# Linear attention and the first half of an FFN in a written order of single steps, and two roots of a double norm as one power

## The chip, the cores and the metric

The kernel runs on one core of one Trainium2 chip. The metric is the time of one execution in microseconds (us). Lower is better. All data are fp32 unless a name says otherwise.

## The reference

The reference is a decoder of two layers over x of 2 x 1024 rows of 256 features: linear attention with an FFN, attention of a short context over the rows' latents, a recurrent cell, causal self-attention, cross-attention, and a mixture of experts. The change lies in the first of these, which is this:

```python
x = x + _L0_attn_ref(_layernorm(x, axis=-1), ...)       # two normalisations follow each other

def _L0_attn_ref(x, ...):
    h = layer_norm(x, ln1_g, ln1_b)                      # (x - mu) * rsqrt(var + 1e-5) * g + b
    q, k, v = heads(h @ wq), heads(h @ wk), heads(h @ wv)    # 4 heads of 64
    q = softmax(q * 64**-0.25, axis=-1)                  # over the 64 features
    k = softmax(k * 64**-0.25, axis=-2)                  # over the 1024 rows
    context = einsum('bhnd,bhne->bhde', k, v)
    x = x + merge(einsum('bhnd,bhde->bhne', q, context)) @ wo + bo
    h = layer_norm(x, ln2_g, ln2_b)
    x = x + gelu(h @ w_ff1 + b_ff1) @ w_ff2 + b_ff2      # 256 -> 1024 -> 256
    return x @ w_d + b_d
```

The double norm needs for each row the factor 1/sqrt(var + eps), called r, and for the second norm 1/sqrt(var * r * r + eps). The product of both is rr, the factor with which the attention's input is scaled.

## The kernel before

The rows of x lie on chip in four blocks of 512 rows (g = 0 to 3; blocks 0 and 1 are batch 0, blocks 2 and 3 batch 1), each as [128, 4, 256]. SP issues the loads in this order: x blocks 0 and 1, the half of w_lin with wk and wv, x blocks 2 and 3, the other half of w_lin (wq, wo), two rows of biases, w_ffn, more rows, and the weights of the two stages after.

`Linear` does the first stage. For each block: `norm` takes statistics on VectorE (`ln_stats`), gets the two roots as powers of -0.5 on POOL (`rsqrt`) with four small VectorE products around the second, writes xh = (x - mean) * rr, turns it by TensorE transposes (`turned`), and scales it into hT, one half on VectorE and the other on ScalarE (`affine`). It also writes h0 = (x - mean) * r, the residual of the attention. For each batch: `keys` multiplies, takes the maximum on VectorE and the exponential on ScalarE into kT; `values` multiplies and copies; `queries` does, for each of two halves, multiply, maximum, subtract, exponential (ScalarE), sum, reciprocal, multiply into the tile qe, then transposes and copies into qT. `context` turns kT back into rows (kr, L353), multiplies it with the values (L363), copies the blocks of the heads into cbd, and multiplies by wo (L375) into wc. `attend` multiplies qT by wc (L393) and adds to h0. `front` is the second norm and its transposes into hT2; `back` is the FFN: eight products of 512 columns each way in four pairs (L441, L427) with Gelu between (L448), the residual (L459), the copy oT (L465), the product with w_d (L474) and the sums into x (L470 for the bias, L482 for the product).

The PSUM memory is handed out as two tiles "s" of 1024 columns, two tiles "t" of 512, and one "f" of 1024. In SBUF, hT, kT and qT share four buffers ("long"); xh, qe and kr share three ("rows4").

What sets the order: the framework plans each engine's instructions itself, except inside a block `tc.manual_schedule()`, where the order of the program is kept. `linear.attention` (batch 0 and 1 up to the attention, and the FFN of block 0), the constants and first loads of `Latent` (the next stage), and `linear.rest` (FFN of block 1 and `front` of blocks 2 and 3) are planned. From then on a manual block follows: `back(2)` and `back(3)`, each alternating step by step with the text and the first batch of `Latent` (`text`, whose first tile is cr, L580 to L649, and `prepare`, whose statistics are at L664). The Latent stage's attention begins after it, with the L769 products. In the planned part the trace has VectorE at block 2's statistics before the second root's small products of block 0.

Of the kernel before, what the change touches and what calls it, by code (L numbers as in the profile page):

```python
# [25 lines left out]
P = 128  # L26
# [197 lines left out]

class Linear:
# [7 lines left out]

    def __init__(self, k, x, w, pool):

        self.k, self.x, self.pool, self.w = k, x, pool, w
        self.h0 = pool.tile([P, NT, D], F32, tag="h0", bufs=1, name="h0")
        self.hT, self.kT, self.vr, self.qT, self.wc, self.ffT = {}, {}, {}, {}, {}, {}

    def long(self, name):  # L240
        return self.own.tile([P, DC, N], F32, tag="long", bufs=4, name=name)

    def four(self, name):
        return self.pool.tile([P, 1024], F32, tag="four", bufs=5, name=name)

    def rows4(self, name):
        return self.own.tile([P, 1024], F32, tag="rows4", bufs=3, name=name)

    def turned(self, rows, out, put):

        k = self.k
        for kc in range(DC):
            tb = k.t()
            for i in range(4):
                k.nc.tensor.transpose(tb[:, i * P : (i + 1) * P], rows[:, i, kc * P : (kc + 1) * P], k.ident)
            put(out[:, kc, :], tb, kc)

    def norm(self, b, half):

        k, x = self.k, self.x  # L260
        g = 2 * b + half
        if half == 0:
            self.hT[b] = self.long("hT")
        rows = lambda i: x[:, 4 * g + i, :]
        mv, r, rr = k.ln_stats(rows, 4, twice=True)
        xh = self.rows4("xh").rearrange("p (t d) -> p t d", d=D)
        for i in range(4):
            k.ln_apply(xh[:, i, :], rows(i), mv, rr, i)
        self.turned(
            xh, self.hT[b][:, :, half * 512 : (half + 1) * 512],  # L270
            lambda out, in_, kc: k.affine(out, in_, k.vec("ln1_g", kc), k.vec("ln1_b", kc), kc),
        )
        for i in range(4):
            k.ln_apply(self.h0[:, 4 * g + i, :], rows(i), mv, r, i)

    def keys(self, b):

        k, nc, w = self.k, self.k.nc, self.w
        scale = 64.0 ** -0.25
        hT = self.hT[b]  # L280
        kT = self.kT[b] = self.long("kT")
        for mc in range(DC):
            s = k.s()
            for nb in range(2):
                for kc in range(DC):
                    nc.tensor.matmul(
                        s[:, nb * 512 : (nb + 1) * 512],
                        lhsT=w["wk"][:, kc, mc * P : (mc + 1) * P],
                        rhs=hT[:, kc, nb * 512 : (nb + 1) * 512],
                        start=(kc == 0),  # L290
                        stop=(kc == DC - 1),
                    )
            m = k.small([P, 1], "k_m")
            nc.vector.tensor_reduce(m, s, AX.X, ALU.max, negate=True)
            nc.vector.tensor_scalar_mul(m, m, scale)
            nc.scalar.activation(
                kT[:, mc, :], s, AF.Exp, bias=m, scale=scale, accum_out=self.ksum[:, b, mc : mc + 1]
            )
        nc.vector.reciprocal(self.ksum[:, b, :], self.ksum[:, b, :])

    def rows_of(self, b, g, name):

        k = self.k
        s = k.s()
        for i in range(4):
            at = (4 * g + i) * P
            for kc in range(DC):
                k.nc.tensor.matmul(
                    s[:, i * D : (i + 1) * D],
                    lhsT=self.hT[b][:, kc, at : at + P],  # L310
                    rhs=self.w[name][:, kc, :],
                    start=(kc == 0),
                    stop=(kc == DC - 1),
                )
        return s

    def values(self, b):
        vr = self.vr[b] = self.own.tile([P, TB, D], F32, tag="vr", bufs=2, name="vr")
        for g in range(2):
            s = self.rows_of(b, g, "wv")  # L320
            self.k.nc.scalar.copy(vr[:, 4 * g : 4 * g + 4, :].rearrange("p t d -> p (t d)"), s)

    def queries(self, b):

        k, nc = self.k, self.k.nc
        scale = 64.0 ** -0.25
        qT = self.qT[b] = self.long("qT")
        for g in range(2):
            s = self.rows_of(b, g, "wq").rearrange("p (h d) -> p h d", d=64)
            qe = self.rows4("qe")  # L330
            q3 = qe.rearrange("p (h d) -> p h d", d=64)
            m, sm = k.small([P, 16], "q_m"), k.small([P, 16], "q_s")
            nc.vector.tensor_reduce(m, s, AX.X, ALU.max)
            nc.vector.tensor_tensor(q3, s, m.unsqueeze(2).to_broadcast([P, 16, 64]), ALU.subtract)
            nc.scalar.activation(qe, qe, AF.Exp, scale=scale)
            nc.vector.tensor_reduce(sm, q3, AX.X, ALU.add)
            nc.vector.reciprocal(sm, sm)
            nc.vector.tensor_tensor(q3, q3, sm.unsqueeze(2).to_broadcast([P, 16, 64]), ALU.mult)
            self.turned(
                qe.rearrange("p (t d) -> p t d", d=D), qT[:, :, g * 512 : (g + 1) * 512],  # L340
                lambda out, in_, kc: k.evac(out, in_),
            )

    def context(self, b):

        k, nc, w = self.k, self.k.nc, self.w
        c, kT, vr = self.cbd[b], self.kT[b], self.vr[b]
        krs = []
        for at in range(0, TB, 4):
            s = k.s()  # L350
            for i in range(4):
                for mc in range(DC):
                    nc.tensor.transpose(  # L353
                        s[:, (i * DC + mc) * P : (i * DC + mc + 1) * P],
                        kT[:, mc, (at + i) * P : (at + i + 1) * P], k.ident,
                    )
            kr = self.rows4("kr")
            k.evac(kr, s)
            krs.append(kr.rearrange("p (t d) -> p t d", d=D))
        t = k.t()  # L360
        for pr in range(DC):
            for i in range(TB):
                nc.tensor.matmul(  # L363
                    t[:, pr * P : (pr + 1) * P],
                    lhsT=vr[:, i, pr * P : (pr + 1) * P],
                    rhs=krs[i // 4][:, i % 4, pr * P : (pr + 1) * P],
                    start=(i == 0),
                    stop=(i == TB - 1),
                )
        for hh in range(2):  # L370
            sl = slice(hh * 64, hh * 64 + 64)
            nc.vector.tensor_copy(c[sl, :, sl], t[sl, : DC * P].rearrange("p (r d) -> p r d", r=DC)[:, :, sl])
        t = k.t()
        for pr in range(DC):
            nc.tensor.matmul(  # L375
                t[:, pr * D : (pr + 1) * D], lhsT=c[:, pr, :], rhs=w["wo"][:, pr, :], start=True, stop=True
            )
        wc = self.wc[b] = self.own.tile([P, DC, D], F32, tag=f"wc{b}", bufs=1, name=f"wc{b}")
        sums = self.ksum[:, b, :]
# [6 lines left out]
    def attend(self, b):  # L386
        k, nc = self.k, self.k.nc
        for g in range(2):
            s = k.s()
            for i in range(4):  # L390
                at = (4 * g + i) * P
                for pr in range(DC):
                    nc.tensor.matmul(  # L393
                        s[:, i * D : (i + 1) * D],
                        lhsT=self.qT[b][:, pr, at : at + P],
                        rhs=self.wc[b][:, pr, :],
                        start=(pr == 0),
                        stop=(pr == DC - 1),
                    )
            four = self.h0[:, 8 * b + 4 * g : 8 * b + 4 * g + 4, :].rearrange("p t d -> p (t d)")  # L400
            nc.vector.tensor_add(four, four, s)

    def front(self, g):

        k = self.k
        h0 = self.h0[:, 4 * g : 4 * g + 4, :]
        rows = lambda i: h0[:, i, :]
        mv, r = k.ln_stats(rows, 4)
        xh = self.four("xh").rearrange("p (t d) -> p t d", d=D)
        for i in range(4):  # L410
            k.ln_apply(xh[:, i, :], rows(i), mv, r, i)
        hT = self.ffT[g] = self.four("hT2").rearrange("p (c n) -> p c n", c=DC)
        self.turned(
            xh, hT, lambda out, in_, kc: k.affine(out, in_, k.vec("ln2_g", kc), k.vec("ln2_b", kc), kc)
        )
# [1995 lines left out]
```

## Time and profile before

| | us |
|---|---|
| median of three runs | 1771.98 |
| lowest and highest of the three | 1766.24 and 1774.56 |
| the profiled execution, its own time | 1776.51 |
| span in the profile, first to last instruction | 1774.4 |
| first TensorE instruction | 13.99 |
| first product of back(2) | 191.17 |
| first product of the Latent attention (L769) | 299.51 |

The profile shows one execution. PE is TensorE's products, PEld its weight loads, DVE is VectorE, ACT ScalarE, POOL GpSimd, SP the engine that issues most loads. An fp32 product has two records on PE, a transpose has one. In the rows of order in time, brackets hold the engine's idle time before the row and what ended it. In the row PEclk, each digit is the granted TensorE clock in a fortieth of the span, in tenths of full speed. In a table of stretches, each row gives the stretch, its length, then for each engine the busy time and the number of instructions, then the granted clock (1.00 is full), the share of the DMA engines that is busy, and GB/s.

### The profile page before, as it was taken

The page shows a single profiled execution, that of the slowest core. Times are in us where ns is not written, and L with a number is a line of the kernel's source. Part 1 is how long each engine was busy: PE and PEld are TensorE (multiplying, and loading weights), DVE is VectorE, ACT ScalarE, POOL GpSimd, SP SyncE. Part 2 cuts the span into 40 slices and gives each one's busy share as a digit, 9 for nine tenths or more (in the row PEclk, how much of TensorE's full clock was granted, in tenths as well). Part 3 has the DMA queues.
Part 4 walks back from the last instruction along what each step waited for, and adds up shares of the span by engine and source line. Part 5 has one row for each costly group of instructions (what it writes and reads, how often), then busy time and mean ns, then how long its engine had stood idle before and what let it go on. Part 6 is the DMA issues. An engine that isn't in the chain of part 4 may idle for free. (4 is left out here: it accounts for less than half of the span.)

```text
span 1774.4 us, 20965 instructions
## 1 busy us (share of the span) xinstructions
PE 1677.3 (95%) x8686; PEld 882.8 (50%) x8686; DVE 804.1 (45%) x1470; ACT 512.7 (29%) x870; POOL 265.7 (15%) x298
## 2 busy tenths in 40 slices
PE   6889899999999799989999999989899999999998
PEld 4655455343343446543433443456546645665566
DVE  5532224845653524467566667366641131111222
ACT  1221232233324132325555445533121111111110
POOL 2010131133213300203111111220000000000420
PEclk9889999999999899969999999999899999999999
DMA  5000000000000100000000000050003122322321
GB/s 225 1 3 1 0 1 4 1 0 1 1 1 1 36 1 0 31 1 1 1 1 1 1 1 1 1 195 2 1 0 107 69 74 71 107 92 81 100 68 48
DMA packets 30550, 59.16 MB, mean 33 GB/s; under 512 B 3640, under 2 KB 23672, under 8 KB 30072
## 3 DMA queue, kind: packets, MB, share of 16 engines
q1 hardware_dynamic: 25512, 50.46, 8.2%
q0 software_dynamic: 1536, 4.20, 0.9%
q10 hardware_dynamic: 3408, 3.17, 0.5%
q8 instruction: 69, 1.13, 0.3%
q14 instruction: 25, 0.20, 0.0%
HBM read 51.00 MB, written 6.82 MB: 33 GB/s over the span
## 5 line engine op out<-in xcount | busy, mean ns | idle before, releaser
L2149 PE MATMUL ps_s<-pair,w 128*128 128x512 f32 (+1 forms) x704 | 304.8, 592 | 0.2 <-ACT pair L2098 0.2
L2149 PEld LDWEIGHTS ps_s<-pair,w 128*128 128x128 f32 (+1 forms) x704 | 130.9, 187 | 164.4 <-issue 163.3
L1338 ACT ACTIVATE pT<-ps_t 128x512 f32<-128x512 f32 (+3 forms) x344 | 150.6, 490 | 149.5 <-PE ps_t L1303 147.7
L1228 PE MATMUL ps_s<-kT,qT 32*128 32x512 f32 (+3 forms) x768 | 182.1, 571 | 10.3 <-DVE part L1244 6.4
L1303 PE MATMUL ps_t<-qT,kT 32*128 32x512 f32 (+3 forms) x688 | 184.3, 554 | 2.2 <-ACT pT L1338 2.2
L2158 DVE TENSOR_TENSOR hid<-ga,ps_s 128x512 f32<-128x512 f32 (+1 forms) x88 | 60.5, 687 | 272.8 <-ACT ga L2157 272.8
L2164 PE MATMUL ps_o<-wo,hid 128*128 128x256 f32 (+1 forms) x704 | 153.5, 379 | 0.0
L1244 DVE TENSOR_REDUCE part<-ps_s 128x2 f32<-128x1024 f32 (+3 forms) x128 | 130.5, 1024 | 45.4 <-PE ps_t L1303 37.3
L2164 PEld LDWEIGHTS ps_o<-wo,hid 128*128 128x128 f32 (+1 forms) x704 | 133.8, 190 | 22.0 <-issue 4.1
L2157 ACT ACTIVATE ga<-ps_s 128x512 f32<-128x512 f32 (+1 forms) x88 | 52.5, 597 | 246.5 <-PE ps_s L2149 246.5
L1228 PEld LDWEIGHTS ps_s<-kT,qT 32*128 32x128 f32 x768 | 61.4, 194 | 86.8 <-issue 46.6
L1268 PE MATMUL ps_o<-pT,vr 128*32 128x256 f32 (+4 forms) x1408 | 99.5, 361 | 1.8 <-POOL pT L1296 1.5
L1296 POOL TENSOR_SCALAR_AFFINE_SELECT pT<-pT 128x256 f32<-128x256 f32 x128 | 51.9, 407 | 319.4 <-ACT pT L1338 310.3
L910 ACT ACTIVATE pT<-ps_s 128x1024 f32<-128x1024 f32 x64 | 65.5, 1023 | 115.4 <-PE ps_s L903 115.4
L2182 POOL DMA_INDIRECT found<-eo_rows,index x32 | 31.9, 997 | 422.5 <-DMA eo_rows<-rows 387.9
L798 DVE TENSOR_REDUCE part<-ps_s 128x2 f32<-128x1024 f32 x64 | 76.4, 1218 | 28.4 <-PE ps_s L791 27.7
L1236 DVE TENSOR_TENSOR ps_s<-ps_s,causal 128x256 f32<-128x256 f32 x128 | 54.9, 429 | 66.5 <-PE ps_t L1303 44.5
L915 POOL TENSOR_TENSOR acc<-acc,pT 128x1024 f32<-128x1024 f32 x24 | 59.4, 2476 | 160.0 <-ACT pT L910 157.3
L1268 PEld LDWEIGHTS ps_o<-pT,vr 128*32 128x32 f32 x1408 | 28.9, 109 | 98.4 <-issue 84.5
L1303 PEld LDWEIGHTS ps_t<-qT,kT 32*128 32x128 f32 x688 | 71.3, 191 | 12.1 <-ACT pT L1338 6.9
L791 PE MATMUL ps_s<-kT,qT 64*128 64x512 f32 x256 | 72.4, 646 | 0.6 <-DVE part L781 0.6
L830 PE MATMUL ps_o<-pT,vr 128*64 128x512 f32 x256 | 69.5, 624 | 0.0
(381 smaller groups left out, 2272.6 us busy)
## 6 DMA issues: line engine op xcount, KB each, us to landing
w<-in_w SPq DMA_DIRECT2D x32, 684.0 KB, 7.1
wo<-in_wo SPq DMA_DIRECT2D x8, 1280.0 KB, 6.9
eo_rows<-rows ACTq DMA_DIRECT2D x12, 256.0 KB, 4.5
w_ffn<-in_w_ffn SPq DMA_DIRECT2D x1, 2304.0 KB, 15.2
x<-in_x SPq DMA_DIRECT2D x4, 512.0 KB, 4.9
w<-in_w_cell SPq DMA_DIRECT2D x2, 1024.0 KB, 16.8
out_x<-x SPq DMA_DIRECT2D x8, 256.0 KB, 2.2
w<-in_w_lat SPq DMA_DIRECT2D x2, 768.0 KB, 16.8
```

Of the source, the lines that this page charges most:

```text
L791: nc.tensor.matmul(s3[:, hh, :], lhsT=q[rows, qt * P : (qt + 1) * P], rhs=kt[rows, half * 512 : (half + 1) * 512], start=True, stop=True,)
L798: nc.vector.tensor_reduce(part[:, half, qt, :], s3, AX.X, ALU.max, negate=True)
L830: nc.tensor.matmul(self.o[hh * 64 : hh * 64 + 64, :], lhsT=self.vr[b][:, kk, h * 64 : (h + 1) * 64], rhs=pT[:, hh, :], start=first, stop=last,
L910: nc.scalar.activation(pT, s3, AF.Exp)
L1228: nc.tensor.matmul(s3[:, hh, :n], lhsT=q[rows, qt * P : (qt + 1) * P], rhs=kt[rows, at : at + n], start=True, stop=True,)
L1244: nc.vector.tensor_reduce(out, s3[:, :, :n], AX.X, ALU.max, negate=True)
L1268: nc.tensor.matmul(self.o[hh * 32 : hh * 32 + 32, cols], lhsT=vr[:, kk, 4 * grp + hh, :], rhs=pts[hh // 2][:, hh % 2, cols], start=first, ...
L1303: nc.tensor.matmul(out, lhsT=kt[rows, kk * P : (kk + 1) * P], rhs=q[rows, j * 512 + q0 : (j + 1) * 512], start=True, stop=True,)
L1338: nc.scalar.activation(pT[:, hh, q0:], heads[hh][:, q0:], AF.Exp)
L2149: nc.tensor.matmul(s[:n, i * 512 : (i + 1) * 512], lhsT=wt[:, kc, at : at + n], rhs=v[:, kc, :], start=(kc == 0), stop=(kc == DC - 1),)
L2158: nc.vector.tensor_mul(hid[:n, hc, :], ga[:n], s[:n, 512:])
L2164: self.k.nc.tensor.matmul(o, lhsT=hid[:n, hc, st * P : (st + 1) * P], rhs=to[:n, hc, :], start=(hc == 0), stop=(hc == len(HCH) - 1),)
```

## The change

`Linear` is rewritten as small methods, each of which issues the instructions of one engine for one block, half or batch, and `attention` calls them in the order of a written list, inside `tc.manual_schedule()`. The list covers all of the stage up to the turned input of block 2: norms, linear attention of both batches, the whole FFN of blocks 0 and 1, and the second norm of blocks 2 and 3. `rest` is gone, so that `Latent`'s constants and first loads come after the list in the program. A name such as `up_03` is the step `up` with arguments 0 and 3. A `drain` of pieces is replaced by the steps up (L441), gelu (L448), down (L427), res (L459), oT (L465), bd (L470), last (L474) and ladd (L482). `turn` with `hT`, `qturn` with `qT` and `fturn` with `fT` are the transposes and their copies; each transposes four tiles for one half of the features. The copies of qT and kr, which took VectorE and ScalarE in turn, are now fixed by `either`. Both roots are computed by one power of [128, 8]: the second four columns are var + eps * (var + eps), whose power -0.5 is r times the second root.

`back(2)` and `back(3)` still alternate with Latent's steps, now written with the same small methods.

```diff
+LINEAR_ORDER = """
+stat_0 mean_0 stat_1 root_0 mean_1 norm_0 root_1 h0_0 turn_00 turn_01 hT_01 hT_00 norm_1 stat_2 turn_11
+turn_10 hT_11 hT_10 h0_1 key_00 stat_3 mean_3 query_00 kmax_00 root_3 kneg_00 mean_2 kexp_00 h0_3 root_2
+val_00 qmax_00 qsub_00 bd_0 qexp_00 key_01 vcopy_00 norm_2 qsum_00 qinv_00 qdiv_00 turn_21 turn_20 hT_21
+kmax_01 val_01 hT_20 kneg_01 bd_1 kexp_01 kinv_0 qturn_001 norm_3 vcopy_01 qturn_000 qT_001 kturn_00
+qT_000 kturn_01 kr_00 turn_30 kr_01 h0_2 turn_31 query_01 hT_31 hT_30 key_10 qmax_01 qsub_01 qexp_01
+ctx_0 qsum_01 qinv_01 qdiv_01 kmax_10 qturn_010 query_10 qT_010 kneg_10 cbd_0 kexp_10 wc_0 qmax_10
+qturn_011 wcs_0 val_10 qT_011 qsub_10 qexp_10 qsum_10 att_01 vcopy_10 qinv_10 qdiv_10 qturn_100 radd_01
+qturn_101 att_00 qT_101 qT_100 fstat_1 fmean_1 froot_1 key_11 radd_00 fnorm_1 fstat_0 fturn_11 val_11
+fmean_0 fT_11 kmax_11 froot_0 kneg_11 fnorm_0 kexp_11 kinv_1 fturn_00 vcopy_11 kturn_10 fT_00 fturn_01
+kr_10 kturn_11 fT_01 up_01 kr_11 up_03 gelu_01 up_05 gelu_03 up_02 gelu_05 up_07 gelu_02 up_04 gelu_07
+up_00 gelu_04 up_06 gelu_00 down_00 gelu_06 fturn_10 query_11 fT_10 up_12 qmax_11 qsub_11 up_13 gelu_12
+qexp_11 down_01 gelu_13 qsum_11 qinv_11 qdiv_11 qturn_111 up_15 qT_111 down_02 gelu_15 up_11 down_03
+gelu_11 res_0 up_17 oT_0 up_10 gelu_17 up_16 gelu_10 down_10 gelu_16 down_11 qturn_110 up_14 qT_110
+ctx_1 gelu_14 down_12 cbd_1 wc_1 down_13 wcs_1 att_11 res_1 radd_11 fstat_3 att_10 oT_1 fmean_3 froot_3
+fnorm_3 last_1 radd_10 fstat_2 fmean_2 fturn_31 ladd_1 froot_2 fturn_30 fT_31 fT_30 last_0 fnorm_2
+fturn_21 ladd_0 fturn_20 fT_21 fT_20
+"""
...
+    def mean(self, g):
+        nc = self.k.nc
+        mv = self.of["mv", g] = self.aggr(self.of.pop(("st", g)), "n")
+        v = self.of["v", g] = self.k.small([P, 8], "n_v")
+        nc.vector.tensor_scalar_add(v[:, :4], mv[:, :, 1], EPS)
+        nc.vector.scalar_tensor_tensor(v[:, 4:], v[:, :4], EPS, mv[:, :, 1], ALU.mult, ALU.add)
+
+    def root(self, g):
+        self.of["r", g] = self.k.rsqrt(self.of.pop(("v", g)), 8)
+
+    def norm(self, g):
+        xh = self.rows4("xh", g)
+        for i in range(4):
+            self.k.ln_apply(
+                xh[:, i * D : (i + 1) * D], self.group(g)[:, i, :], self.of["mv", g], self.of["r", g][:, 4:], i
+            )
...
+    def qsub(self, b, g):
+        m, s = self.of.pop(("q_m", b, g)), self.of.pop(("q_s", b, g)).rearrange("p (h d) -> p h d", d=64)
+        self.k.nc.vector.tensor_tensor(
+            self.heads(b, g), s, m.unsqueeze(2).to_broadcast([P, 16, 64]), ALU.subtract
+        )
+
+    def qexp(self, b, g):
+        qe = self.of["qe", (b, g)]
+        self.k.nc.scalar.activation(qe, qe, AF.Exp, scale=self.scale)
...
+    def either(self, out, in_, i):
+        if i:
+            self.k.nc.scalar.copy(out, in_)
+        else:
+            self.k.nc.vector.tensor_copy(out, in_)
...
     def attention(self, own):
...
-        for half in range(2):
-            self.norm(0, half)
-        self.keys(0)
-        self.values(0)
-        self.queries(0)
-        for half in range(2):
-            self.norm(1, half)
-        self.context(0)
-        self.keys(1)
-        self.attend(0)
-        self.values(1)
-        self.queries(1)
-        self.front(0)
-        self.context(1)
-        self.front(1)
-        drain(self.back(0))
-        self.attend(1)
-
-    def rest(self):
-
-        drain(self.back(1))
-        for g in range(2, 4):
-            self.front(g)
+            self.blocks.append(c)
+        for step in LINEAR_ORDER.split():
+            name, args = step.rsplit("_", 1)
+            getattr(self, "h0_" if name == "h0" else name)(*(int(a) for a in args))
...
-                linear.attention(ap)
+                with tc.manual_schedule():
+                    linear.attention(ap)
...
-            k.tiny = lp
-            linear.rest()
             k.tiny = early
```

## The prediction

> **What bounds the kernel now.** I read the page's head first, then the busy time of four stretches, then the order of time on TensorE, and last VectorE and ScalarE beside it.
>
> ```profile
> PE 1677.3 (95%) x8686; PEld 882.8 (50%) x8686; DVE 804.1 (45%) x1470; ACT 512.7 (29%) x870; POOL 265.7 (15%) x298
> ...
> PEclk9889999999999899969999999999899999999999
> ...
> 0.00:13.99 13.99, 0.00 (x0) 0.03 (x1) 6.22 (x30) 1.28 (x1) 5.16 (x16) 1.00 0.88 299
> 13.99:191.17 177.18, 159.80 (x616) 106.77 (x616) 76.59 (x183) 38.14 (x51) 16.41 (x25) 0.94 0.08 34
> 191.17:299.51 108.34, 102.17 (x318) 55.43 (x319) 28.39 (x51) 35.70 (x50) 26.48 (x10) 0.94 0.01 2
> ```
>
> TensorE is the bound. All that the change writes anew lies in the first two stretches: 13.99 us in which TensorE has nothing, then 177.18 us of linear attention and the FFN of blocks 0 and 1. There TensorE is idle for 177.18 - 159.80 = 17.4 us, and its clock averages 0.94.
>
> ```profile
> 13.99 2.10 PE L255 MATMUL ps_t<-ident,xh 128*128 128x128 f32 x8 [13.99 <-POOL rs_y L144]
> 33.48 10.63 PE L308 MATMUL ps_s<-w_lin,hT 128*128 128x256 f32 x48 [1.96 <-ACT kT L296]
> 43.94 1.04 PE L353 MATMUL ps_s<-ident,kT 128*128 128x128 f32 x8
> 47.77 1.94 PE L353 MATMUL ps_s<-ident,kT 128*128 128x128 f32 x8 [2.79 <-DVE qe L334]
> 77.91 13.98 PE L308 MATMUL ps_s<-w_lin,hT 128*128 128x256 f32 x64
> 95.55 1.94 PE L353 MATMUL ps_s<-ident,kT 128*128 128x128 f32 x8 [2.79 <-DVE qe L334]
> 101.30 1.94 PE L255 MATMUL ps_t<-ident,qe 128*128 128x128 f32 x8 [1.44 <-DVE qe L338]
> 124.11 3.60 PE L441 MATMUL ps_t<-hT,w_ffn 128*128 128x512 f32 x8
> 189.06 1.31 PE L255 MATMUL ps_t<-ident,xh 128*128 128x128 f32 x8 [2.23 <-DVE xh L183]
> 191.17 6.73 PE L441 MATMUL ps_t<-hT,w_ffn 128*128 128x512 f32 x8 [0.79 <-DVE hT L134]
> ```
>
> The columns are start, duration, work, and in brackets the idle time before it with what ended it. Two things cost time. First, waits for VectorE inside the query softmax (qe). Second, what follows them: eight transposes take 1.94 us where they took 1.04, and eight products of 512 columns 6.73 us where they took 3.60.
>
> ```profile
> 10.53 0.43 DVE L164 BATCH_NORM_STATS2 ln_st<-x 128x6 f32<-128x256 f32 x1 [2.23 <-DMA x<-in_x]
> 13.04 0.16 DVE L179 TENSOR_TENSOR ln_rr<-rs_y,rs_y 128x4 f32<-128x4 f32 x1 [0.90 <-POOL rs_y L144]
> 114.37 1.28 ACT L448 ACT_TABLE_LOAD   x1
> ```
>
> VectorE stands at the statistics of block 2, whose x has not landed, while block 0 waits behind them for its second root.
>
> **TensorE's work is unchanged; what is it at full clock?** From undisturbed rows: 16 records of 256 columns 3.46 us (13.98 for 64), 8 of 512 columns 3.43 (start to start), four transposes 0.45, a context 3.9, wc 0.95. Keys 4 x 3.43 = 13.7; values, queries and attend 12 x 3.46 = 41.5; 32 groups of four transposes 14.4; context and wc 9.7; FFN of two blocks: up and down 2 x 27.4, res and last 2 x 5.25, so 65.3. Sum 144.6. So of the 177.2 us, 17.4 are idle and 159.8 - 144.6 = 15.2 are slow clock.
>
> Here a rule differs. The Trainium skill, "TensorE: Matmul & The Clock Gate", Part 1, says that the array falls to half clock after an idle window of about 3.4 us. No idle stretch inside this stage is longer than 2.79 us, so by the rule the 15.2 us would not be the waits' doing and would stay. The rows show half speed straight after waits of 2.79 and 2.23 us (and none after 1.96), so I take the row: removing those waits removes the slow clock too. By the rule the forecast below would be about 12, not 27, us.
>
> **The start.** Statistics of block 0 end at 6.1 as now, mean and two small operations at 6.7, one power of 128x8 on POOL 1.7 us (the 128x8 row, L144, has 1.69; 128x4 has 1.05), ready at 8.45. VectorE does block 1's statistics meanwhile, until 8.6, then norm_0: first slice at 9.0, first transpose at 9.1 instead of 13.99. The second power, three small products and block 2's statistics are out of the way. Gain 4.9. Then h0_0 to 11.3, hT_00 to 12.1, norm_1 to 13.4, stat_2 to 14.7 (x landed by 10.5), hT_10 to 15.5. TensorE is paced by this and cold: key_00 ends near 19, with 5.2 us of work done since 9.1, so 4.7 are lost. In total POOL does 4 roots of 1.7 for 8 of 1.05, and VectorE runs 12 operations of at most 0.16 us fewer, all small.
>
> **The written order.** A query's softmax takes 1.22 + 1.22 + 1.06 + 1.21 + 0.24 + 1.22 = 6.2 us before its transposes. Now only kturn, 0.9 us, lies ahead of the wait at 47.77. In the order, TensorE has this between query and qturn: query_00: val_00, key_01, turn_2, val_01, 11.2 us; query_01: key_10, ctx_0, 7.3; query_10: wc_0, qturn_011, val_10, att_01, 8.3; query_11: up_12, up_13, down_01, 6.9. I walked the list with these durations, each engine in order, with two s, two t and one f buffers. qdiv is ready at 30.2, 47.75, 60.65 and 105.45; TensorE gets there at 33.9, 48.9, 61.3 and 104.8. Slack 3.7, 1.1, 0.65, and a wait of 0.7. The s buffers come free 1 to 7 us before they are asked for (key_01 at 26.0, qsub_00 done at 25.0). VectorE is busy for some 48 of the 52 us from 9 to 61, so this stretch is balanced to a microsecond. Other waits in the walk: up_05 for gelu_01's buffer 0.4, last_0 for ladd_1 0.3, fturn and fT at the seam to back(2) 1.1 (ladd_0 is queued ahead of fT_20), scattered 0.6. With the 0.7, 3.1. Stage: 144.6 + 4.7 + 3.1 = 152.4, so back(2) starts near 161.5 instead of 191.17: 29.7 earlier, the 4.9 included.
>
> **Added: two table loads.** gelu_12, qexp_11, gelu_13 alternate Gelu and Exp, so ScalarE loads its table three times instead of once, 1.28 us each by the row above. They are hidden: from up_12's end ScalarE needs 0.69 + 1.28 + 1.06 + 1.28 + 0.69 = 5.0 us, TensorE has 5.15 (up_13, down_01); the 0.7 wait above contains the first load. Without cover they cost 2.6. The skill, "ScalarE: Activation LUTs", What ACT_TABLE_LOAD costs, speaks against the change: 2.66 us a switch with the drain, advising to group by set. By that, qturn_111 and the buffer of up_15 would wait about 2.7 us instead of 0.7. The row shows no drain (Gelu starts at 115.67, 1.30 after the load's start), so I keep 0.7 and leave 2 to the range.
>
> **Moved: what follows.** back(2) starts 0.8 us after a busy TensorE, so its first eight records take 3.5 instead of 6.73: 3.2 more. The Latent stage's constants and text loads use freed memory. SP now issues the first, cr, at 97.58, after a wait of 85.2 us for L353. At worst they now wait for att_10, the last reader of the attention's tiles, near 151: six issues (3.3 us together) and 3.0 to land, 157.5, before VectorE has done with the block at 161.5. POOL's memsets, 5.8 us at 110.96, would lie at 151 to 157 with froot_2 behind them, up to 2.4 late; last_0 (3.46 us) covers this. cr's norm needs some 3 us of VectorE and POOL after fT_20; up_20 and up_21 (3.4) cover it, just. Without cover, 2 to 4 us at the seam. No load of weights moves; SP has none waiting behind.
>
> **Sum.** 29.7 + 3.2 = 32.9 at best. From that I take 6 for what the walk cannot see: 48 us of VectorE with under 1.2 us of slack at most places, where a tenth more is 5 us, and the seam. 27 us. The profiled execution took 1776.51 (span 1774.4), so it would become about 1749.5; it lies 4.5 above the median of the three runs, 1771.98, and against that I forecast 1745.
>
> **Rivals.** *Half of it.* The order is tight and VectorE's hand-offs miss by half a microsecond in a score of places; a wait of over 2 us then brings the slow clock back. For: the slacks of 1.1 and 0.65. Against: the hand-offs in the trace are short (cbd's copy starts 0.04 us after its product's end). 10 to 19 us gained, about 1757.
>
> *Given back at the seam.* Constants, mask loads and text land in TensorE's way, or the order gains nothing because the planner's order was held by data and not by its choices. For: cr waits 85 us for memory now. Against: the wait on block 2's statistics and the bare query chains are choices of order. 0 to 9 us, about 1768.
>
> *Slower: VectorE becomes the bound.* Beside two-input adds on POOL (L204), VectorE's L470 takes 3.37 us for 1.22 and L740 4.43 for 2.28. If powers and memsets did that from 9 to 61 us, 48 us of VectorE at a factor of 1.9 are 43 us more: 1788. It decides from a factor of 1.75 on, (27 + 9) / 48 = 0.75 more. Against: POOL has some 7 us of short powers in that stretch, and VectorE's slices beside today's powers keep 0.41 us.
>
> **How the numbers follow.** Forecast 0.72, half 0.18, given back 0.06 (one third of it still over 0.5%), slower 0.04. Half a percent, 8.9 us, is about what a measurement of this kernel can tell from no change. Faster 0.72 + 0.18 + 0.02 = 0.92, same 0.04, slower 0.04. Range: at best 33 us and 5 for the scatter of the median, 1734; on the slow side to the slow end of half, 1762.
>
> **What would show it.** First transpose near 9 us; back(2)'s first product at 158 to 168; busy TensorE in between near 150, idle under 8, clock 0.97 or more; no wait for qe over 1 us; three table loads before the latent stage; four powers of 128x8. Wrong if TensorE waits in many places for hT, qe or fxh, if the slow clock stays without the waits, or if the stretch from back(2) to the first L769 product grows beyond its 108.3 us.

## The result, and the profile after

The kernel after takes 1742.51 us (median of four runs, 1742.2 to 1744.03), the kernel before on the same chip 1773.03 (four runs, 1766.24 to 1774.56). The ratio is 0.983, with a 95% interval of 0.9809 to 0.9852: 30.5 us between the medians. The profiled executions took 1776.51 and 1744.03, so 32.5 apart.

TensorE's clock, from the page of the kernel after:

```profile
PEclk9999999999999799989999999999899999999999
```

The same four stretches as before, cut at the same events (first transpose, first product of `back(2)`, first product of the Latent attention, end). The engines stand in the order PE, PEld, DVE, ACT, POOL:

```profile
0.00:9.22 9.22, 0.00 (x0) 0.00 (x0) 4.49 (x23) 1.28 (x1) 4.01 (x15) 1.00 0.78 244
9.22:167.71 158.49, 151.50 (x616) 102.76 (x617) 80.53 (x175) 40.69 (x53) 15.40 (x23) 0.98 0.13 50
167.71:271.83 104.12, 97.94 (x319) 53.94 (x320) 29.55 (x55) 35.70 (x49) 26.51 (x10) 0.98 0.01 2
271.83:1742.20 1470.37, 1407.60 (x7746) 717.07 (x7751) 692.70 (x1207) 437.64 (x769) 217.63 (x247) 0.98 0.10 33
```

| stretch | before | after | difference |
|---|---|---|---|
| start to first transpose | 13.99 | 9.22 | 4.8 |
| to `back(2)` | 177.18 | 158.49 | 18.7 |
| to the Latent attention | 108.34 | 104.12 | 4.2 |
| to the end | 1474.89 | 1470.37 | 4.5 |
| span | 1774.4 | 1742.2 | 32.2 |

Of the 32.2 us, 27.7 are won where the change was made and in `back(2)` behind it. In the stage, the 616 records of TensorE are the same; it is idle for 158.49 - 151.50 = 7.0 us where it was 17.4, and busy for 151.5 where it was 159.8, at a clock of 0.98 for 0.94.

The last 4.5 us lie in stages that no line of the change touches. The experiments below come back to them.

In the order of time on TensorE, these rows of the kernel after hold its waits in the stage:

```profile
9.22 2.30 PE L302 MATMUL ps_t<-ident,xh 128*128 128x128 f32 x8 [9.22 <-DVE xh L183]
12.62 2.21 PE L302 MATMUL ps_t<-ident,xh 128*128 128x128 f32 x8 [1.10 <-DVE xh L183]
...
44.92 3.73 PE L469 MATMUL ps_t<-kr,vr 128*128 128x128 f32 x32
48.49 0.60 PE L302 MATMUL ps_t<-ident,qe 128*128 128x128 f32 x4
...
103.90 0.63 PE L302 MATMUL ps_t<-ident,qe 128*128 128x128 f32 x4 [0.95 <-DVE qe L434]
...
150.63 3.62 PE L590 MATMUL ps_f<-w_ffn,oT 128*128 128x256 f32 x16
158.81 6.78 PE L590 MATMUL ps_f<-w_ffn,oT 128*128 128x256 f32 x16 [3.69 <-DVE x L600]
167.71 3.67 PE L539 MATMUL ps_t<-hT,w_ffn 128*128 128x512 f32 x8 [1.25 <-DVE hT L134]
```

The waits are 1.10 + 0.95 + 3.69 + 1.25 = 7.0, which is all the idle time there is. The two waits of 2.79 us for a query's softmax are gone: the context's products (44.92) run straight into the transposes of qe (48.49). One large wait is left, at 158.81, before the step `last_0`. That step's 16 records then take 6.78 us where its twin `last_1`, at 150.63, takes 3.62. This pair of rows is what the experiments are mostly about.

### The profile page after: what moved, and what is told of

It is laid out like the page before. It is cut to its first block, busy times and chain, and to the rows that moved or that the text cites. A ratio compares the mean times of both kernels' runs of the same rounds, so it can differ in the third digit from the quotient of the medians.

```text
span 1742.2 us, 20929 instructions
## 1 busy us (share of the span) xinstructions
PE 1657.0 (95%) x8679; PEld 873.8 (50%) x8686; DVE 807.3 (46%) x1458; ACT 515.3 (30%) x872; POOL 263.5 (15%) x294
## 5 line engine op out<-in xcount | busy, mean ns | idle before, releaser
L1345 PE MATMUL ps_s<-kT,qT 32*128 32x512 f32 (+3 forms) x768 | 178.1, 553 | 11.2 <-DVE part L1361 7.2
L915 DVE TENSOR_REDUCE part<-ps_s 128x2 f32<-128x1024 f32 x64 | 76.4, 1218 | 28.4 <-PE ps_s L908 27.7
```

The costliest lines, as they stand in the source:

```text
L915: nc.vector.tensor_reduce(part[:, half, qt, :], s3, AX.X, ALU.max, negate=True)
L1345: nc.tensor.matmul(s3[:, hh, :n], lhsT=q[rows, qt * P : (qt + 1) * P], rhs=kt[rows, at : at + n], start=True, stop=True,)
```

## The experiments

All versions are timed against the kernel before on the same chip. Its median was 1773.03 to 1775.93 in the several sets, so versions are compared by their ratios. The time at which x lands differs from run to run by up to 1 us (block 0's statistics start at 4.72 to 5.71), so the stage is measured from its own first transpose:

| version | first transpose | to `back(2)` | to Latent attention | from there to the last product | ratio |
|---|---|---|---|---|---|
| before | 13.99 | 177.18 | 285.52 | 1469.9 | |
| after | 9.22 | 158.49 | 262.61 | 1465.4 | 0.983 (0.9809 to 0.9852) |
| the list, two roots | 10.28 | 157.84 | 261.92 | 1467.5 | 0.9838 (0.9816 to 0.986) |
| before, one root | 10.58 | 172.90 | 278.65 | 1473.4 | 0.9969 (0.9957 to 0.998) |
| the list, planned | 11.13 | 156.80 | 262.38 | 1465.3 | 0.9838 (0.9813 to 0.9863) |
| constants later | 9.20 | 151.93 | 256.18 | 1476.3 | 0.9825 (0.98 to 0.985) |
| `ladd_1` first | 9.66 | 154.69 | 259.88 | 1470.7 | 0.9812 (0.9796 to 0.9829) |
| 24 fillers | 10.17 | 154.39 | 258.66 | 1471.6 | one run, 1747.09 us |
| 32 fillers | 9.17 | 154.61 | 259.83 | 1472.6 | 0.9822 (0.9801 to 0.9843) |
| `stat_2` early | 13.68 | 156.95 | 262.51 | 1463.6 | one run, 1746.27 us |
| bare query | 10.01 | 161.56 | 267.03 | 1463.3 | one run, 1747.05 us |
| constants later, Exp first | 9.63 | 152.18 | 256.44 | 1474.4 | 0.9811 (0.979 to 0.9833) |
| after again | 9.36 | 156.95 | 262.51 | 1463.4 | 0.9808 (0.979 to 0.9825) |
| idle products before `back(2)` | 9.45 | 158.69 | 262.88 | 1471.7 | 0.9831 (0.9813 to 0.9849) |

The middle columns come from one profiled execution each. The rows "after" and "after again" are the same kernel, and show how far such numbers repeat: within 1.5 us for `back(2)`, 0.1 for the Latent attention, 2.0 for the rest.

### Which half of the change did it

Three versions take the change apart. In the first, the list stays and the two roots come back.

```diff
-        v = self.of["v", g] = self.k.small([P, 8], "n_v")
-        nc.vector.scalar_tensor_tensor(v[:, 4:], v[:, :4], EPS, mv[:, :, 1], ALU.mult, ALU.add)
+        v = self.of["v", g] = self.k.small([P, 4], "n_v")
...
-        self.of["r", g] = self.k.rsqrt(self.of.pop(("v", g)), 8)
+        nc.gpsimd.tensor_tensor(r, self.of.pop(("v", g)), self.k.minus_half[:, :4], ALU.pow)
+        nc.vector.tensor_mul(u, r, r)
+        nc.vector.tensor_mul(u, u, mv[:, :, 1])
+        nc.vector.tensor_scalar_add(u, u, EPS)
+        nc.gpsimd.tensor_tensor(r2, u, self.k.minus_half[:, :4], ALU.pow)
```

> The kernel after, with both roots taken one after the other again (two powers of 128x4, three small VectorE operations between, one behind), in the same written order. Theory 'order' (the gain is waits of TensorE and the slow clock behind them, taken away by the order): xh of block 0 comes about 1.2 us later, first transpose near 10.4 instead of 9.2, and some 2 us of small VectorE work lie in a stretch where it is nearly full; 2 to 5 us over the kernel after, about 1746. Theory 'roots' (the single power brings more than half of the 30 us): over 1757.

It took 1746.44 us (1743.27 to 1747.97). The first transpose came 1.06 us later than in the kernel after, and the Latent attention was reached 0.4 us later. Within the list, one power for two is worth about 1 us at the start. Whether that microsecond lasts, these two profiles cannot tell: `last_0` took 5.41 us here and 6.78 in the kernel after, behind the same wait (the bare query below shows why). The gain of some 30 us is not the roots'.

In the second, the kernel before gets the single power and nothing else.

```diff
-        mv, r, rr = k.ln_stats(rows, 4, twice=True)
+        v = k.small([P, 8], "n_v")
+        k.nc.vector.tensor_scalar_add(v[:, :4], mv[:, :, 1], EPS)
+        k.nc.vector.scalar_tensor_tensor(v[:, 4:], v[:, :4], EPS, mv[:, :, 1], ALU.mult, ALU.add)
+        r = k.rsqrt(v, 8)
+        rr = r[:, 4:]
```

> The kernel before, with the one change that both roots are one power of 128x8; the planner orders the rest. Theory 'order': the second power and its products go from the start's chain, 1 to 5 us off, 1768 to 1772, while the waits for qe and the slow clock behind them stay. Theory 'roots': 1758 or less.

It took 1769.92 us, 6.0 less than the kernel before in the same set. VectorE's order of time shows what one power alone cannot mend, and the waits of TensorE in the stage (total, times, longest) show what it leaves:

```profile
9.78 0.43 DVE L267 BATCH_NORM_STATS2 n_st<-x 128x6 f32<-128x256 f32 x1 [1.17 <-DMA x<-in_x]
...
PE ps_t L255 <- DVE xh L183: 12.8, 2, 10.6
PE ps_s L362 <- DVE qe L343: 5.6, 2, 2.8
PE ps_t L255 <- DVE qe L347: 4.0, 4, 1.7
```

VectorE still stands at block 2's x until 9.78, so the first transpose comes at 10.58. Both waits of 2.8 us for qe are there. By one profile each, the power alone brings 3.4 us at the start and 10.3 by the Latent attention; the list alone brings 27.3 by then, and both together 27.7. The two overlap almost wholly: the list removes what made the second root late.

In the third, the list is kept as the program's order, but the framework plans the stage again.

```diff
-                with tc.manual_schedule():
-                    linear.attention(ap)
+                linear.attention(ap)
```

> The kernel after, with the list's steps issued in the same program order but not inside the manual block, so that the planner may reorder them. Theory 'order': the planner brings back waits, clock 0.97 or less, 1750 to 1772. Theory 'splitting' (small steps in this program order are enough, pinned or not): within 3 us of the kernel after, 1742.

It took 1745.69 us (1741.28 to 1750.6); its ratio cannot be told from that of the kernel after. The planner moved one thing back that matters, block 2's statistics, and VectorE waited for its x as before:

```profile
10.33 0.43 DVE L290 BATCH_NORM_STATS2 n_st<-x 128x6 f32<-128x256 f32 x1 [1.79 <-DMA x<-in_x]
```

That made the first transpose 1.9 us later. From there to the Latent attention it took 262.38, against 262.61 pinned. My expectation, that the planner would undo the order, was wrong. Once the stage is written in single steps in a good order, planning it or pinning it comes to nearly the same. No version has the single steps in the old order, so the share of the splitting by itself is not shown; the next two versions measure two places of the order.

### The start: does the order of `stat_2` matter by itself?

```diff
-stat_0 mean_0 stat_1 root_0 mean_1 norm_0 root_1 h0_0 turn_00 turn_01 hT_01 hT_00 norm_1 stat_2 turn_11
+stat_0 mean_0 stat_1 root_0 mean_1 stat_2 norm_0 root_1 h0_0 turn_00 turn_01 hT_01 hT_00 norm_1 turn_11
```

> The kernel after, with stat_2 (statistics of block 2, whose x lands near 10.5) moved ahead of norm_0, where the planner had it in the kernel before. Theory 'start' (the wait for x in VectorE's queue is the larger part of the first 4.8 us): first transpose near 12.2 instead of 9.2, first product of back(2) 2.5 to 4 us later than 167.7. Rival (the second root was the larger part): under 1.5 us later.

VectorE's order of time in this version:

```profile
11.90 1.41 DVE L290 BATCH_NORM_STATS2 n_st<-x 128x6 f32<-128x256 f32 x4 [2.25 <-DMA x<-in_x]
```

The first transpose came at 13.68, about where it was before (13.99) and 4.5 us later than in the kernel after. Part of that is a late transfer. VectorE waits here for block 2's x, which landed at 11.9 (issued at 3.2, 8.7 us to landing); in the kernel after it landed at 10.1 (2.4 and 7.7). With x there at 10.1 the order would cost 4.5 - 1.8 = 2.7 us, an estimate from these figures. The edit puts all four slices of block 2's statistics ahead, where the planner of the kernel before had one; the planned list above, with one ahead, lost 1.9 us. The loss is not made up for later: from the first transpose on the stage is as long as in the kernel after (262.51 and 262.61). One operation that waits for a transfer, put ahead of another that doesn't, cost 2 to 3 us of the span.

### A bare query: is the slow clock the wait's doing?

The context's products are taken out from between query and qturn and put behind; four idle transposes stand in their place.

```diff
-ctx_0 qsum_01 qinv_01 qdiv_01 kmax_10 qturn_010 query_10 qT_010 ...
+fill_4 qsum_01 qinv_01 qdiv_01 kmax_10 qturn_010 ctx_0 query_10 qT_010 ...
```

> The kernel after, with ctx_0 moved from before qturn_010 to behind it, and four transposes of the identity in its old place: TensorE then waits for the query softmax of qdiv_01 about 2.6 us, as in the kernel before. By the row of the kernel before, the products behind the wait run at half clock for some 3 us, so that the next stretch is 5 to 6 us late in all and back(2) starts near 173. By a rule that needs 3.4 us of idle time, only the wait itself is lost, and back(2) starts near 170.5. If the order of the queries does not matter, within 1 us of 167.7.

TensorE's order of time there, for the rows 44.92 and 48.49 of the kernel after:

```profile
48.48 0.85 PE L302 MATMUL ps_t<-ident,qe 128*128 128x128 f32 x4 [2.69 <-DVE qe L440]
49.13 5.18 PE L475 MATMUL ps_t<-kr,vr 128*128 128x128 f32 x32
```

The wait is 2.69 us, and the work behind it runs slowly: 0.85 for 0.60, and 5.18 for 3.73, together 1.7 us. Counted from the first transpose, `last_1` starts 4.4 us later than in the kernel after (145.84 for 141.41): 2.7 of wait and 1.7 of clock. At `back(2)` only 3.1 us are left, where 5 to 6 were expected, because `last_0` takes 5.41 us here and 6.78 in the kernel after. The Trainium skill ("TensorE: Matmul & The Clock Gate", Part 1) puts the fall of the clock at an idle window of about 3.4 us; here 2.69 were enough. So the row was the better guide than the rule as the prediction had read it, but the slow clock after one such wait is worth 1.7 us, less than the expectation's row.

The granted clock shows how the two belong together. Here are TensorE's stretches around that wait (busy time of PE first, clock third from the end):

```profile
45.33:48.74 3.41, 0.72 (x8) 0.52 (x7) 3.10 (x4) 0.21 (x1) 0.00 (x0) 1.00 0.00 0
48.75:52.15 3.40, 3.40 (x19) 3.40 (x18) 1.38 (x3) 1.21 (x2) 0.00 (x0) 0.50 0.00 0
```

The clock fell at 48.74, 0.26 us after the wait was over, and rose 3.41 us later. In each of the 14 profiles the clock changes only on a grid of steps of 3.41 us, and it stays low for one to seven whole steps (the last stay is cut off by the end of the profile). In this part of the kernel it fell at the end of a step in which TensorE was idle for more than half the time, wherever the wait lay in it:

| profile and wait | step, us | TensorE busy in it, us | clock in the next step |
|---|---|---|---|
| before, 1.96 | 30.06 to 33.47 | 1.46 | 1.00 |
| before, 2.79 | 43.71 to 47.12 | 1.27 | 0.50 |
| bare query, 2.69 | 45.33 to 48.74 | 0.72 | 0.50 |
| constants later, 1.44 | 152.25 to 155.66 | 1.97 | 1.00 |
| `ladd_1` first, 1.87 | 153.59 to 157.00 | 1.54 | 0.50 |
| after, 3.69 | 154.80 to 158.20 | 0.32 | 0.50 |
| the list, two roots, 3.68 (first part) | 155.14 to 158.54 | 1.77 | 1.00 |
| the same wait (second part) | 158.55 to 161.96 | 1.38 | 0.50 |

Up to 300 us, the 30 steps before a fall were busy for at most 1.54 us; the other steps at full clock were busy for at least 1.77, all but the one in the first row. In later stages the clock also fell after steps that are busier by this count. So the length in the skill is there in the traces, but the window need not be empty, and what a wait costs depends on how it lies on the grid: behind one and the same wait of 3.69 us, `last_0` took 5.41 us in three profiles and 6.27 to 6.78 in four.

### The seam: what holds `last_0`?

VectorE, POOL and the summary of the tile fxh in the kernel after (for a tile: shortest, median and longest of one instruction in ns):

```profile
149.85 4.27 DVE L183 TENSOR_SCALAR fxh<-h,f_mv,rs_y 128x256 f32<-128x256 f32 x4 [1.12 <-POOL rs_y L144]
157.56 1.19 DVE L600 TENSOR_TENSOR x<-x,ps_f 128x1024 f32<-128x1024 f32 x1
...
151.08 1.85 POOL L671 MEMSET mparts<- 128x1024 bf16 x2
...
L183 DVE TENSOR_SCALAR fxh<-h,f_mv,rs_y x8: 394/404/3212, 149.9 to 160.4; 128x256 f32<-128x256 f32 x8
```

`last_0` waits for the one f buffer, which `ladd_1` (L600) frees at 158.75. On VectorE, `ladd_1` stands behind `fnorm_3`, whose four slices take 4.27 us where such groups take 1.37 elsewhere. The summary counts the eight slices of two blocks: half of them take some 0.4 us or less, and one takes 3.21. That slice begins at 150.91 and ends at 154.12, while POOL goes through its row of constants (the memsets of `Latent`, from 149.77 to past 153.98). Four versions test this.

*Constants later.* The memsets move behind the text's last step; two short ones stay.

```diff
+    def constants(self):
...
+        self.constants()          # behind the text's last step
```

> The kernel after, with Latent's constants other than kbd and vbd (4.4 us of POOL memsets and selects, now at 149.8 to 154.6 and 158.7) written behind the text of the Latent stage, near 195 us. Theory 'shared access' (POOL's memsets slow the four VectorE operations of fnorm_3 from 1.37 to 4.27 us, so ladd_1 is late, last_0 waits 3.7 us and runs at half clock): fnorm_3 about 1.4 to 2 us, the wait before last_0 under 1.2 us and last_0 at 3.6 us; back(2) starts 4 to 7 us earlier, 1736 to 1739. Rival 'queue' (ladd_1 is late because of its place behind radd_10 and fstat_2 alone): fnorm_3 stays at 4 us and the time at 1742.

VectorE and TensorE in that version:

```profile
148.57 2.02 DVE L183 TENSOR_SCALAR fxh<-h,f_mv,rs_y 128x256 f32<-128x256 f32 x4 [1.12 <-POOL rs_y L144]
...
155.28 3.72 PE L590 MATMUL ps_f<-w_ffn,oT 128*128 128x256 f32 x16 [1.44 <-DVE x L600]
```

`fnorm_3` takes 2.02 us beside the 1.0 us of memsets that are left, the wait shrinks from 3.69 to 1.44, and `last_0` runs at full clock. The Latent attention comes 6.4 us sooner (256.18 for 262.61). The seam's cause is confirmed, and it costs what it looked like: 6.4 us. Yet the whole time is 1746.03 us (ratio 0.9825), no better than the kernel after: the stages behind took 1476.3 us for 1465.4.

*`ladd_1` first.* It is moved ahead of `radd_10` and block 2's second statistics.

```diff
-fnorm_3 last_1 radd_10 fstat_2 fmean_2 fturn_31 ladd_1 froot_2 ...
+fnorm_3 last_1 ladd_1 radd_10 fstat_2 fmean_2 fturn_31 froot_2 ...
```

> The kernel after, with ladd_1 (the sum that frees the one f buffer for last_0) moved in the list ahead of radd_10, fstat_2 and fmean_2. fnorm_3 still lies beside POOL's memsets and takes about 4.3 us. If the late buffer is what TensorE waits for, last_0 starts near 155.5 instead of 158.8 and at full clock, and the first product of back(2) comes 4 to 6 us earlier than 167.7, the first L769 product likewise than 271.8. If the wait only moves on (fnorm_2 becomes late, as radd_10 is now behind ladd_1), less than 2 us.

The memsets still hold `fnorm_3` for 4.27 us. The wait falls to 1.87 us, `last_0` takes 5.41, and the Latent attention comes 2.7 us sooner: less than expected, because the slow clock follows this shorter wait as well (it lies within one step of the grid).

*Fillers.* TensorE gets idle transposes to do ahead of `last_0`, first 24 of them.

```diff
-... fT_31 fT_30 last_0 fnorm_2
+... fT_31 fT_30 fill_24 last_0 fnorm_2
...
+    def fill(self, n):
+        s = self.k.s()
+        for i in range(n):
+            at = i % 8 * P
+            self.k.nc.tensor.transpose(s[:, at : at + P], self.k.ident, self.k.ident)
```

> The kernel after, with 24 transposes of the identity into an s buffer, which nobody reads, ahead of last_0, where TensorE now waits 3.7 us. No work is earlier by this. Theory 'slow clock follows the wait': last_0 takes 3.5 to 3.8 us instead of 5.4 to 6.8, and back(2) starts 2 to 3 us earlier than 167.7. Rival (the clock falls for another reason): last_0 stays over 5 us and nothing is earlier.

```profile
151.10 1.46 DVE L183 TENSOR_SCALAR fxh<-h,f_mv,rs_y 128x256 f32<-128x256 f32 x4 [1.12 <-POOL rs_y L144]
...
152.33 2.02 POOL L680 MEMSET mparts<- 128x1024 bf16 x2
...
158.82 3.62 PE L596 MATMUL ps_f<-w_ffn,oT 128*128 128x256 f32 x16
```

`last_0` takes 3.62 us, but this run could not tell: `fnorm_3` took 1.46 and not 4.27, so `ladd_1` was done at 157.66 and the wait would have been some 1.4 us by itself, which is as short as the one that brought no slow clock with the constants later. Instead it showed something else. The fourth slice began 0.17 us ahead of the mparts memsets, exactly as in the kernel after, and here it ran through in 0.40 us, while the memsets took 2.02 us for 1.85. In each of the two runs one engine waited for the other, and it was not the same one. So the fillers were lengthened to 32 (`fill_24` becomes `fill_32`):

> The list with 32 idle transposes (3.7 us at full clock) ahead of last_0. With 24 of them the seam did not show what it was built for: fnorm_3 took 1.46 us there and not 4.27, so the wait would have been only some 1.4 us by itself, which another version has shown to bring no slow clock. The slices show why: in the kernel after, three of fnorm_3's four slices take 0.4 us and the fourth, begun 0.17 us ahead of POOL's first bf16 memset, stands 3.21 us until POOL's row of memsets is through; in the fill of 24 the same slice began 0.17 us ahead of the same memset and ran 0.40, and the memsets took 2.02 for 1.85. Theory of a toss between the two engines, the loser waiting: either length can come, 4.27 as in eight runs of nine. If 4.27 comes: by the theory that the slow clock follows the idle wait, last_0 takes 3.6 right after the filler and the FFN of block 2 starts 155.2 to 155.6 us after the first transpose (158.49 in the kernel after); if the slow clock has another cause, last_0 takes 5.4 to 6.8 and it starts at 157 to 158.5. If 1.46 comes again, the filler itself makes last_0 some 2.3 us late, the FFN of block 2 starts near 155.3 by that alone, and the short length belongs to this program and not to chance. Whole time within the scatter of the kernel after, 1740 to 1747.

```profile
148.98 4.27 DVE L183 TENSOR_SCALAR fxh<-h,f_mv,rs_y 128x256 f32<-128x256 f32 x4 [1.12 <-POOL rs_y L144]
...
154.08 3.66 PE L311 MATMUL ps_s<-ident 128*128 128x128 f32 x32
157.93 3.72 PE L596 MATMUL ps_f<-w_ffn,oT 128*128 128x256 f32 x16 [0.19 <-DVE x L606]
```

Here the slice stood again (4.27), the wait was filled but for 0.19 us, and `last_0` took 3.72 us. Work that computes nothing made the next 16 records 1.7 to 3.1 us faster (3.72 for 5.41 to 6.78 in the seven profiles that wait here for 3.69 us), and `back(2)` starts 154.61 us after the first transpose, 3.9 sooner than in the profile after and 2.3 sooner than in its repetition. The slow clock at the seam is the wait's doing. By the Latent attention 2.8 us of this are left, against 6.4 with the constants moved: the fillers take away the slow clock alone, the moved constants most of the wait too.

### Exp first

ScalarE's three table loads stay, but `qexp_11` goes ahead of `gelu_12`, so that the wait for qe at 103.90 might shrink; this was put on top of the later constants.

```diff
-... up_12 qmax_11 qsub_11 up_13 gelu_12 qexp_11 down_01 gelu_13 ...
+... up_12 qmax_11 qsub_11 up_13 qexp_11 gelu_12 down_01 gelu_13 ...
```

> The kernel after, with Latent's constants written later as in e4 and with qexp_11 ahead of gelu_12 in the list, so that ScalarE loads the Exp table while it waits and TensorE's wait for qe of 0.95 us goes. Distance from the first transpose to the first L769 product: 262.6 us in the kernel after, 256.2 in e4; here 255 to 255.6. If the end of the kernel follows the start of the Latent attention, it is 6 to 8 us faster than the kernel after on the same chip; if the slow-clock periods in the untouched stages depend on where they fall, anything from 8 us faster to 2 us slower.

ScalarE in that version, and then in the kernel after:

```profile
98.01 1.28 ACT L422 ACT_TABLE_LOAD   x1 [9.20 <-DVE qe L416]
```

```profile
98.61 1.28 ACT L422 ACT_TABLE_LOAD   x1
99.91 1.06 ACT L422 ACTIVATE qe<-qe 128x1024 f32<-128x1024 f32 x1
100.98 1.28 ACT L549 ACT_TABLE_LOAD   x1
102.27 0.69 ACT L549 ACTIVATE fT<-ps_t,vecs 128x512 f32<-128x512 f32 x1
```

The load did not run ahead: it waited with its exponential for `qsub_11`, 9.20 us. Nor had `gelu_12` stood in the way: in the kernel after it ends at 98.60 and `qsub_11` at 98.61. The exponential begins 1.30 us after the end of `qsub_11` there (99.91) and 1.37 us after it here (97.93 and 99.30); that it stands 0.6 us further up is the shift of all that lies ahead of it. The wait for qe was 1.03 us, and the stage was 256.44 us long, for 256.18 without this edit. The expectation was wrong. The whole time is 1743.56 us (1736.58 to 1747.3).

### Where the seam's microseconds go

Five versions win 2.7 to 6.4 us by the Latent attention and none of them is shown to be faster in the end. In the table, the profiled executions fall into two groups for the untouched rest: 1463 to 1468 us with a granted clock of 0.976 to 0.978 over the span, and 1470 to 1476 with 0.968 to 0.970. The kernel before (1469.9) and its version with one root (1473.4) lie in the second by their rest. To see whether the code makes the group, the kernel after was run again, and once with 28 idle transposes behind `fT_20`, which moves all that follows a little and changes nothing else.

```diff
-fturn_21 ladd_0 fturn_20 fT_21 fT_20
+fturn_21 ladd_0 fturn_20 fT_21 fT_20 fill_28
```

> The kernel after once more, unchanged, as the measure for the others on this chip: ratio to the kernel before 0.983 within 0.002.

> The kernel after, with 28 transposes of the identity that nobody reads (some 3.1 us, of which 1.2 fill a wait) ahead of back(2); all that follows is moved by about 1.9 us and otherwise the same. If what follows takes the same time wherever it falls, the time is 1.9 us over the kernel after on this chip. If the slow-clock periods in the untouched stages depend on where they fall, it differs by other than that, by -4 to +6 us, and the clocks of the same stages differ between the two profiles.

The kernel after again: 1742.22 us (1738.05 to 1743.75), clocks of 0.976 to 0.979. With the idle transposes: 1750.67 and 1749.59 at clocks of 0.968 and 0.969, and 1743.18, 1743.64 and 1743.7 at 0.977. One and the same program falls into both groups, 6.5 us apart. The 32 fillers do so too: 1748.28 and 1747.89 at 0.970, 1740.09 and 1742.68 at 0.979 and 0.978. A place where it happens is a stretch of the causal attention; here is first the kernel after again, then the version with idle products:

```profile
730.00:760.00 30.00, 25.06 (x140) 12.09 (x144) 23.93 (x34) 6.96 (x17) 3.27 (x8) 0.78 0.00 1
```

```profile
730.00:760.00 30.00, 25.68 (x105) 11.68 (x104) 19.83 (x25) 7.21 (x14) 2.45 (x6) 0.60 0.00 0
```

The clock of the stretch is 0.78 in one and 0.60 in the other, with 140 records of TensorE in the same 30 us in one and 105 in the other. It is enough to hide 6 us won elsewhere, and it is also the likeliest home of the last 4.5 us in the table of the result: the nine timed runs of the kernel after all have clocks of 0.976 to 0.979, while of the 42 timed runs of the kernel before that have a clock on record only two reach 0.973 (1767.29 and 1767.62 us). That it was the change that put it there is not shown.

What decides between the groups is open, but the 14 profiles give a hint: the place of the grid of 3.41 us. The first product of the Latent attention begins 0.98 to 1.01 or 2.93 to 3.02 us behind an edge of it in the six profiles of the better group, and 3.20 to 3.31 or 0.38 to 0.49 us in the eight of the other. The grid is not tied to the program: in the two profiles of the kernel after its edges fall 1.19 and 2.69 us behind the first instruction. This was read off afterwards, and no version sets the place on purpose, so it is not shown to be the cause.

## Why the prediction was right, point by point

- **The start.** First transpose foretold at 9.1, measured 9.22. The reason holds, with a correction of shares: the order (`stat_2` behind `norm_0`) carries 1.9 us of it by the planned list and some 2.7 by the `stat_2` version, and the second root 1.06. Measured apart they don't add up to the 4.8, since in the kernel before the second root stood behind the wait for x.
- **The query's softmax.** Slacks of 3.7, 1.1 and 0.65 us and one wait of 0.7 were foretold. There were no waits in the first three and one of 0.95.
- **The slow clock follows the waits.** Foretold from the rows of 2.79 and 2.23 us. The bare query (2.69), the later constants (1.44, full clock) and the 32 fillers bear it out. What the prediction did not see is the grid: it set the length of the wait against the rule's window, where the idle share of a step of 3.41 us decides.
- **Table loads.** Three before the Latent stage, Gelu starting 1.29 us after its load, as foretold; no drain shows in the rows.
- **`back(2)`'s first records.** 3.5 us foretold, 3.67 measured (6.73 before); the whole stretch to the Latent attention is 4.2 us shorter.
- **The step that was mis-sized: the seam.** The sum had a wait of 0.3 us of `last_0` for `ladd_1`; it was 3.69, and `last_0` took 6.78 for 3.46. That is 3.4 + 3.3 = 6.7 us, and `back(2)` started at 167.71 for 161.5, 6.2 late. The prediction saw that POOL's memsets would come to lie at 151 to 157 and asked only what they do to POOL's own queue (`froot_2`). It did not ask what VectorE does beside them. The mechanism stood among the rivals, at a place where it did not happen: from 9 to 61 us the groups of four slices keep 1.36 to 1.38 us.
- **The allowance of 6 us** "for what the walk cannot see" was meant for VectorE's small delays and the seam. The seam took all of it, so the sum came out: 27 foretold, 27.7 by the Latent attention. That the two were of one size was luck.
- **Not foretold:** the 4.5 us in the stages behind. With them the medians lie 30.5 us apart, for a forecast of 1745 that was measured as 1742.51.
- **Rivals.** Neither half of it nor a gain given back at the seam occurred. The notion in the second, that the planner's order may be no worse, was right in another way than meant: planning the same list gives nearly the same time.

## What to carry to other kernels

Between a product and the transpose that needs its softmax, put other work of the bounding engine, as long as the chain takes: laying one query bare again cost 4.4 us, wait and slow clock together. Writing the steps in that order was enough, pinned or not. When moved code changes which memory comes free when, look up everything that this releases, memsets too, and ask beside which instructions of the other engines it will run. Measure an edit by its own stage first: the whole time carried 6 us of clock that the edit did not own.

## What the hardware showed that was not expected

- A four-slice VectorE group took 4.27 us for 1.37 in nine of the ten runs that have the full row of memsets beside it, and 1.46 in one. It is not a slowdown: one slice stands for 2.8 us through several POOL instructions in a row. The Trainium skill ("SBUF — State Buffer", Who interferes with whom) describes a port pair that one of the two engines holds for a whole instruction while the other blocks. The trace agrees that one blocks, and adds that the loser here was passed over by one POOL instruction after the other, and that equal starts (0.17 us apart in both) ended either way. Whether that is chance or belongs to the one program (24 fillers) is open.
- A granted clock that changes only on a grid of 3.41 us, and fell after 30 of the 31 steps in the first 300 us that TensorE spent idle for more than half. Waits of 1.87, 2.69 and 3.69 us and, before, of 2.23 and 2.79 brought it down, one of 1.44 did not; the one of 1.96 before is the exception.
- A table load that carries the wait of its exponential (9.20 us).
- One program at 1743.5 and at 1750 us, with the granted clock at 0.977 and 0.968.
